# Taking both groups of heads for each half of the queries, in every block of a stack of graph attention layers

## The chip, the cores and the metric

The kernel runs on one core of one Trainium2 chip. Its time is the device time of one execution in microseconds (us). The profile is one execution of the program, recorded by the hardware profiler. PE is the matmul engine (PEld is its weight loading), DVE, ACT and POOL are the vector, scalar and GpSimd engines, and SP is the queue that issues nearly all DMAs here.

## The reference

Sixteen batches `x` of 1024 nodes with 128 features pass through three transformer layers whose attention is masked by one adjacency matrix, and then through one graph attention layer:

```python
# layers 0, 1, 2 (B=16, N=1024, 8 heads of 16)
Q, K, V = h @ Wq, h @ Wk, h @ Wv
scores = einsum('bnhd,bmhd->bhnm', Q, K) / sqrt(16)
attn = softmax(where(adj == 0, -inf, scores))
x = layer_norm(h + (einsum('bhnm,bmhd->bnhd', attn, V) @ Wo + bo), ln1_g, ln1_b)
x = layer_norm(x + relu(x @ W1 + b1) @ W2 + b2, ln2_g, ln2_b)
# layer 3
h = x @ W
e = leaky_relu((h @ a_src)[:, :, None] + (h @ a_dst)[:, None, :], 0.2)
out = layer_norm(softmax(where(adj == 0, -inf, e)) @ h + x)
```

## The kernel before

**Blocks and steps.** One block is the attention of one batch in one of the three layers; there are 48. The list `blocks` (line 651) takes four batches at a time: layer 0 of all four, layer 1 of all four, layer 2 of all four, then the next four batches. A block has 32 steps. A step (`score_step`, line 411) is four heads (one of two groups `g`) for one half of the queries (`qh`, 512 of 1024) against one tile of 128 keys (`kt`, 0 to 7). It makes the scores of two heads at a time on PE (line 419) into one of three PSUM slots; then either ACT takes the exponential (426) and POOL multiplies by the mask (427), or DVE adds the mask (429) and ACT takes the exponential (441). Which of the two depends on `kt` alone. Four steps later PE multiplies the exponentials with the values into one accumulator (line 446). After eight steps the accumulator of that (g, qh) is complete; `finish` (449) transposes it on DVE (457), takes reciprocals (459) and scales on POOL (460) into the tile `A`, which has one part for each half of the queries.

**The order in a block.** Before, the loops run group 0 with both halves, then group 1 with both halves; only the first and the last block run half 0 with both groups and then half 1 with both groups (line 757).

**Stacking.** PE multiplies in a form in which each float32 of a query or key is split in two parts, `hi` and `lo`. `split` (372) makes them from the projections, and `stack(m, g)` (397) lays rows of them into the tiles that line 419 reads: two tiles Wk and two Wq for a group of heads, each filled by 4 DMAs of 128 KB on SP (line 404). So one `stack` is 16 DMAs. The tags Wk and Wq have 4 buffers each: those of both groups of a block. A buffer can be filled again only when its last score matmul has read it.

`stack(m, 1)` is written at step 1 of block m (step 6 in block 0), `stack(m + 1, 0)` at step 19 of block m (step 24 in block 0); ahead of that line the projections of block m + 1 must have been made (`need(("proj", m + 1))`, line 781).

**What else runs in the steps.** Each step may also run one small task (`piece`, 682) from chains with due times: the projections of the next block (`proj_tasks`), what follows attention in the block before (`post_tasks`: transposing `A` at 473, output projection, two layer norms, feed-forward), and the last layer of a finished batch (`last_tasks`). In the last layer `rows_gh` (577) issues 16 small DMAs on SP (lines 589 and 590) whose rows the edge matmuls of line 603 read eight or more steps later, and `end` (630) issues the output (635).

**Who sets the order.** PE and ACT run in the order in which the code writes their instructions (line 754). The orders of DVE, POOL and SP are made by a planner at build time, which works with its own estimates of how long instructions take; at run time each engine and queue takes its own list strictly in that order. A DMA on SP that waits for a buffer holds up all DMAs behind it.

## Time and profile before

| | us |
|---|---|
| median of three runs | 4116.18 (4115.72 to 4121.67) |
| the profiled execution | 4115.92, its span 4114.1 |
| PE busy, weight loads apart | 3809.8 (93%) |
| DVE, ACT, POOL busy | 3405.7 (83%), 3393.8 (82%), 3445.6 (84%) |
| stacking DMAs issued by SP | 1536 of 128 KB |
| mean granted clock of PE | 0.98 of full speed |

A busy share is an average over the whole span. In ordinary blocks (76 us each, 2.4 us a step) a step needs about 0.66 us of PE for scores and 0.98 us for values, and the tasks fill the rest. Blocks that also carry the last layer take 80 to 102 us. In the views below, a line of the order in time gives start, duration, engine, line, operation, tiles and count, and in brackets how long the engine stood idle before and whom it waited for; a line of the waits gives total, number and longest.

### The profile page before, as it was taken

What the parts mean: (1) busy time and instruction counts of PE and PEld (TensorE: products, weight loads), DVE (VectorE), ACT (ScalarE), POOL (GpSimd) and SP (SyncE); (2) the same over time, 40 slices, a digit from 0 to 9 for tenths busy, and PEclk for the clock granted to TensorE, in tenths of its full rate; (3) what the DMA queues carried; (4) which work ended last, traced back from release to release, by engine and by line L of the source; (5) the groups of instructions that cost most, each with busy time, mean ns of one, the idle gap of its engine ahead of it and who ended that gap; (6) DMA issues with size and microseconds to landing.
All of it is one profiled execution on the core that took longest, in us unless ns stands there. A gap on an engine that the chain in (4) does not pass through costs nothing.

```text
span 4114.1 us, 107861 instructions
## 1 busy us (share of the span) xinstructions
PE 3809.8 (93%) x44501; PEld 1545.5 (38%) x44501; DVE 3405.7 (83%) x5326; ACT 3393.8 (82%) x3961; POOL 3445.6 (84%) x3010
## 2 busy tenths in 40 slices
PE   7999999999999999999999999999999999999996
PEld 2333333344443333334444333333434433333445
DVE  6888888888887888888888888888888888888874
ACT  7999999977778999997777899998777789999760
POOL 5888888888888888887888888888888888888884
PEclk8999999999999999999999999999999999999997
DMA  6221222222211221221222221221222112222100
GB/s 158 61 63 48 57 63 54 51 53 59 64 51 50 63 63 48 57 63 48 59 54 55 61 60 45 63 63 43 53 74 54 48 47 58 62 54 51 51 20 19
DMA packets 124465, 233.13 MB, mean 57 GB/s; under 512 B 34624, under 2 KB 73792, under 8 KB 123968
## 3 DMA queue, kind: packets, MB, share of 16 engines
q1 hardware_dynamic: 122960, 225.71, 21.9%
q8 instruction: 354, 5.80, 0.6%
q14 instruction: 143, 1.17, 0.1%
q10 hardware_dynamic: 1008, 0.44, 0.0%
HBM read 15.54 MB, written 8.39 MB: 6 GB/s over the span
## 4 chain that ended last, share of the span: by engine, by line
PE 49%; DVE 19%; ACT 12%; POOL 11%; issue 9%; ACTq 0%; DMA 0%; SPq 0%; DVEq 0%; POOLq 0%
PE t L293 19%; PE acc L446 15%; PE s L419 12%; DVE e L429 11%; POOL e L427 6%; ACT e L426 5%; ACT e L441 5%; DVE st L318 2%; PE t L282 2%; DVE lo L382 1%; POOL x L337 1%; DVE x L325 1%; ACT xT L287 1%; DVE tt L457 1%; POOL x L341 1%
## 5 line engine op out<-in xcount | busy, mean ns | idle before, releaser
L429 DVE TENSOR_TENSOR e<-s,mask_add 128x1024 f32<-128x1024 f32 x2112 | 2499.5, 1211 | 406.7 <-PE s L419 321.1
L441 ACT ACTIVATE e<-e 128x1024 f32<-128x1024 f32 x2112 | 2196.5, 1062 | 365.0 <-DVE e L429 340.0
L427 POOL TENSOR_TENSOR e<-e,mask 128x1024 f32<-128x1024 f32 x960 | 2048.6, 2149 | 391.3 <-ACT e L426 376.8
L446 PE MATMUL acc<-e,v 128*17 128x512 f32 x12288 | 1628.5, 602 | 63.4 <-DVE tt L457 32.6
L419 PE MATMUL s<-Wq,Wk 64*128 64x512 f32 x6144 | 1206.6, 458 | 83.4 <-ACT e L426 34.6
L426 ACT ACTIVATE e<-s 128x1024 f32<-128x1024 f32 x960 | 982.3, 1023 | 190.9 <-PE s L419 174.7
L419 PEld LDWEIGHTS s<-Wq,Wk 64*128 64x128 f32 x6144 | 499.3, 185 | 1068.9 <-DVE e L429 430.6
L446 PEld LDWEIGHTS acc<-e,v 128*17 128x17 f32 x12288 | 208.0, 95 | 578.6 <-issue 463.6
L337 POOL TENSOR_SCALAR x<-x,mv 128x128 f32<-128x128 f32 x896 | 389.2, 448 | 24.0
L341 POOL TENSOR_TENSOR x<-x,ln_g 128x1024 f32<-128x1024 f32 x97 | 229.3, 2364 | 33.3 <-PE t L282 33.3
L293 PE MATMUL t<-hd,e 128*32 128x129 f32 x8192 | 243.3, 276 | 4.7 <-DVE x L621 3.2
L335 POOL TENSOR_TENSOR mv<-mv,half_neg 128x4 f32<-128x4 f32 x224 | 231.9, 1035 | 18.5
L293 PEld LDWEIGHTS t<-hd,e 128*32 128x32 f32 x8192 | 226.1, 110 | 23.1 <-DVE x L325 4.9
L325 DVE TENSOR_TENSOR x<-t,x 128x512 f32<-128x512 f32 x192 | 131.7, 686 | 91.6 <-PE t L293 90.7
L293 PE MATMUL t<-x1T,W 128*32 128x512 f32 x1536 | 203.9, 603 | 3.0 <-ACT x1T L287 1.5
L318 DVE BATCH_NORM_STATS2 st<-x 128x6 f32<-128x128 f32 x896 | 196.7, 279 | 3.0
L282 PE MATMUL t<-identf,x 128*128 128x128 f32 x888 | 147.2, 289 | 55.2 <-DVE lo L382 27.2
L293 PEld LDWEIGHTS t<-W,hT 128*32 128x32 f32 x6144 | 172.5, 111 | 63.6 <-issue 26.3
L333 POOL TENSOR_SCALAR mv<-mv 128x4 f32<-128x4 f32 x224 | 52.8, 236 | 164.0 <-DVE mv L320 136.3
L293 PE MATMUL t<-W,hT 128*32 128x128 f32 x6144 | 187.1, 274 | 2.7 <-DVE x L325 1.9
L282 PEld LDWEIGHTS t<-identf,x 128*128 128x128 f32 x888 | 94.6, 142 | 250.0 <-issue 93.7
L606 DVE SCALAR_TENSOR_TENSOR e<-s,mask 128x1024 f32<-128x1024 f32 x128 | 150.5, 1209 | 4.8 <-PE s L603 4.1
(97 smaller groups left out, 2488.2 us busy)
## 6 DMA issues: line engine op xcount, KB each, us to landing
Wk<-hi SPq DMA_DIRECT2D x384, 128.0 KB
Wk<-lo SPq DMA_DIRECT2D x384, 128.0 KB
Wq<-hi SPq DMA_DIRECT2D x384, 128.0 KB
Wq<-lo SPq DMA_DIRECT2D x384, 128.0 KB
x<-in_x_dram SPq DMA_DIRECT2D x16, 512.0 KB
out_dram<-x SPq DMA_DIRECT2D x31, 256.0 KB
ai<-in_adj_dram SPq DMA_DIRECT2D x8, 512.0 KB
g_rows<-parts SPq DMA_DIRECT2D x120, 4.0 KB
```

The source lines that it names most:

```text
L282: nc.tensor.transpose(ps[:, t * P:(t + 1) * P], src[:, 4 * h + t, :], identf)
L293: nc.tensor.matmul(dst[j:j + SLOT, :], lhsT[:, j:j + SLOT], rhs, start=start, stop=stop)
L318: nc.vector.bn_stats(st[:, t, :], z[:, t, :])
L335: nc.gpsimd.tensor_tensor(v, v, half_neg[:, ts], OP.pow)
L337: nc.gpsimd.tensor_scalar(z[:, t, :], z[:, t, :], mv[:, t, 0:1], mv[:, t, 1:2], op0=OP.add, op1=OP.mult)
L341: nc.gpsimd.tensor_mul(z, z, rows(gain, n))
L419: nc.tensor.matmul(ps[:, r * 512:(r + 1) * 512], k[64 * r:64 * r + 64, kt * P:(kt + 1) * P], q[64 * r:64 * r + 64, q0:q0 + 512], start=Tru ...
L426: nc.scalar.activation(ev, psv, AF.Exp, scale=HD ** -0.5)
L427: behind["pool"] = nc.gpsimd.tensor_mul(ev, ev, m).ins
L429: behind["dve"] = nc.vector.tensor_add(ev, psv, m).ins
L441: nc.scalar.activation(ev, ev, AF.Exp, scale=HD ** -0.5)
L446: nc.tensor.matmul(acc[j * SLOT:j * SLOT + HD + 1, :], v_bufs[m % 2][:, kt, 2 * j + g, :], e[:, j, :], start=first, stop=last)
```

## The change

Every block now runs half 0 of the queries with both groups of heads and then half 1 with both, as the first and last block did. The `stack` of the next block's group 0 is written at step 24 in every block, five steps later than before in all but the first.

```diff
             order = [(g, qh) for g in range(G) for qh in range(2)]
-            if m in (0, len(blocks) - 1):
+            if True:
                 order.sort(key=lambda x: x[1])
...
-                    if at == (24 if m == 0 else 19):
+                    if at == 24:
                         need(("proj", m + 1))
                         stack(m + 1, 0)
```

## The prediction

> **What bounds the kernel now.** I read the busy line of the page first, then busy time by stretch (one ordinary block, then blocks 12, 13 and 14), then the waits of the DMA queue, and last the order in time on SP and PE. A step's place in time comes from PE's score matmuls (L419): 6144 of them, four to a step, in order, so the first of each four starts a step. I number blocks from 0 and the 32 steps of a block from 0.

> ```profile
> PE 3809.8 (93%) x44501; PEld 1545.5 (38%) x44501; DVE 3405.7 (83%) x5326; ACT 3393.8 (82%) x3961; POOL 3445.6 (84%) x3010
> ...
> 561.21:637.32 76.11, 71.65 (x724) 25.63 (x721) 65.36 (x97) 69.46 (x79) 66.97 (x57) 1.00 0.23 57
> 1062.70:1157.17 94.47, 89.00 (x1314) 42.93 (x1314) 79.93 (x139) 69.86 (x88) 75.55 (x73) 1.00 0.21 55
> 1157.17:1256.60 99.43, 93.34 (x1361) 44.16 (x1360) 81.03 (x136) 74.48 (x85) 82.76 (x77) 1.00 0.23 58
> ...
> SPq L404 <- PE s L419: 2018.2, 141, 32.7
> ```

> The columns of a stretch are its length and then PE, PEld, DVE, ACT, POOL busy. An ordinary block takes 76.1 us with PE busy 71.6; blocks 13 and 14, which also carry the last layer of earlier batches, take 94.5 and 99.4 with PE idle 5.5 and 6.1. So PE, fed in an order written by hand, sets the pace, and what stops PE costs time. The last line is the one that this change touches: SP, which issues the stacking DMAs (L404), stands at the head of its queue waiting for PE's score matmuls 141 times, 2018 us in all. The stacks are issued as soon as their target buffers are free, not when the loop reaches the line that writes them.

> [...]the tiles of step 0's first scores had their last issue end at 17.46 us and were read at 19.69 (at most 2.2 us), and those of its second scores had it end at 22.58 and were read at 25.53 (2.95 us, the wait named as a DMA). I take 2.2 for a landing and keep 2.95 as its upper end. [...]so a late stack stops all of PE. The trace agrees: in the 2.95 us wait above no other matmul ran. SP keeps its list in order too, as the views below show.

> **The change part by part.**

> *(a) Order of the halves.* The 32 steps do the same matmuls, masks and exponentials (which engine masks depends on kt alone). 46 blocks take them in another order. Removed 0, added 0. The four "finish" tasks still come at steps 11, 19, 27 and 35. Following the due times of the task chains by hand, every other task falls on the same step as before: none is forced earlier by the need for the projections at step 19 (their last piece falls at 18), so asking at 24 forces nothing either.

> *(b) When the buffers come free.* Tags Wk and Wq have 4 buffers, 2 per group of heads. Group 0's were last read at step 15 and are now last read at step 23. Group 1's still at step 31. So the next block's first stack starts 8 steps later (the written line moves 5 steps; the buffers decide).

> *(c) When the stacks are needed.* First stack: at step 32, as before. Second stack: at step 8 of its block, where it was 16.

> A stack is 16 DMAs on SP. In an ordinary block (here 5 into 6):

> ```profile
> 444.03 0.47 SPq L404 DMA_DIRECT2D Wk<-hi  x1
> ...
> 483.61 0.47 SPq L404 DMA_DIRECT2D Wk<-hi  x1
> ...
> 493.19 1.24 SPq L404 DMA_DIRECT2D Wq<-lo  x2
> ...
> 464.10 0.74 PE L419 MATMUL s<-Wq,Wk 64*128 64x512 f32 x4
> ...
> 485.08 0.73 PE L419 MATMUL s<-Wq,Wk 64*128 64x512 f32 x4
> ...
> 501.12 1.04 PE L419 MATMUL s<-Wq,Wk 64*128 64x512 f32 x4
> ```

> The three PE lines are steps 23 and 32 (= step 0 of block 6) and step 8. The second stack runs from 483.61 to 494.43, 10.8 us (median over the trace 11.0), so 0.67 us a DMA. New first stack: free at 464.8, issued by 476, landed by 478.2; needed at 485.1: 6.9 us spare. Second: landed by 494.43 + 2.2 = 496.6 (497.4 at 2.95); needed at 501.1: 3.7 to 4.5 spare; the tightest block has 6.4 us from last issue to step 8, so 3.4 to 4.2. Ordinary blocks: cost 0, hidden by PE's steps 23 to 31 and 0 to 7.

> *(d) The blocks with other work on SP.* Of the four groups of batches, three have heavy blocks after them (10 to 14, 22 to 26, 34 to 38). Each batch's last layer issues 16 small DMAs (rows_gh, L589/L590), 10.6 us of SP, and in-order. They come at steps 10, 16, 23 and 26 of blocks 10, 11, 12 and 13 (and so on by 12). At 10 and 16 SP is done with them by about step 22, before the stack is released. At 23 and 26 they now meet it, where before the stack had run at steps 15 to 20. Measured:

> ```profile
> 1042.08 0.74 PE L419 MATMUL s<-Wq,Wk 64*128 64x512 f32 x4
> ...
> 1061.30 0.77 PE L603 MATMUL s<-g_rows,h_rows 4*128 4x256 f32 x8
> ...
> 1063.83 0.50 PE L419 MATMUL s<-Wq,Wk 64*128 64x512 f32 x2 [0.63 <-DVE e L606]
> ...
> 1045.30 0.68 SPq L589 DMA_DIRECT2D g_rows<-parts  x1
> ...
> 1055.31 0.60 SPq L590 DMA_DIRECT2D h_rows<-parts  x1
> ...
> 1147.69 0.69 SPq L589 DMA_DIRECT2D g_rows<-parts  x1
> ```

> Which goes first is the planner's choice. Block 11 shows how it chooses:

> ```profile
> 927.49 0.59 SPq L404 DMA_DIRECT2D Wk<-lo  x1
> 930.67 0.69 SPq L589 DMA_DIRECT2D g_rows<-parts  x1
> ...
> 941.03 0.60 SPq L590 DMA_DIRECT2D h_rows<-parts  x1
> 941.67 1.16 SPq L404 DMA_DIRECT2D Wq<-hi  x2
> ```

> Four stack DMAs, then all sixteen of rows_gh (SP stood still 2.6 us for them), then the other twelve. What the fifth stack DMA reads was ready before the rows' data (ACT writes both in order, one step apart), so the planner counted an issue longer than it takes: four from step 15's release to the rows' readiness at step 17.4.

> *Block 12 (24, 36).* Release at 1042.08 + 0.74 + 0.2 = 1043.0. At that planner's pace three stack DMAs precede the rows (ready 1.3 steps later): rows from 1045.3 to 1055.9, the other 13 by 13 x 0.65 = 8.4, to 1064.3, landed 1066.5. The second scores of step 32 ran at 1063.83: 2.7 us late.

> *Block 13 (25, 37).* Step 23 began at 1136.3, release 1137.3; the rows are ready 10.4 us later, eight planned issues. Eight real ones end at 1142.5, SP stands until 1147.69, rows to 1158.6, eight more to 1163.8, landed 1166.0; the second scores of step 32 would have run at 1157.5: 8.5 us late. The second stack follows at once and lands by about 1177, step 8 being at 1183: no cost. Block 14's output and x DMAs (0.4 us each) meet 12 us of spare.

> Sum: 3 x (2.7 + 8.5) = 34 us of PE standing still. Of this the 5.5 to 6.1 us that PE idles in the following block can be regained at most, for PE runs ahead only as far as three score buffers: between 17 and 34 us remain. I take 24: 4114.1 + 24 = 4138 in the profile's terms. The profiled execution took 4115.9 and the median is 4116.2, so 2 more: **4140**.

> **Rivals.**

> *Stack first.* If all 16 of it precede the rows, block 13 has no stall (stack ends at 1148.3), and block 12 has stack to 1054.0, rows to 1064.7, landed 1066.9, against edge matmuls at 1061.30: 5.6 us, three times, 17 us at most; 10 after regain: 4126. For it: the release comes before the rows' data in both blocks. Against: block 11's order.

> *Hidden.* All of it fits: 4116 within 8 us. For it: ordinary blocks have the spare shown, and blocks 13 and 14 may lose their stall to waits that they have anyway. Against: in block 12, 32 DMAs from 1043.0 cannot land before 1066 in any order. This is also the case where the change does nothing.

> *Faster.* The first half's attention is complete after the finish at step 19, not 27, so its transpose (L473, 0.70 us on DVE, at 411.06 in block 5, in a stretch where DVE has no pause) can go to steps 20 to 25, where DVE waits for PE (6.9 us a block). Bound 0.70 x 47 = 33 us: 4083. It decides if DVE alone holds PE at steps 0 to 5. Against: ACT does two 1.06 us exponentials a step there, 2.1 us, more than DVE's share.

> *Planner worse.* It sees stacks longer than they are (above), so at steps 0 and 8 it plans with PE standing and may order DVE and POOL worse in heavy blocks, which exceed ordinary ones by 91 us a group. A tenth to a quarter of 273 us: 27 to 68 on top of the forecast, 4165 to 4210.

> **How the numbers follow.** Interleaved 0.34 (4128 to 4155), stack first 0.24 (4116 to 4134), hidden 0.17, faster 0.15, planner worse 0.10. 0.2% is 8 us, about what a measurement of this kernel can tell from no change (its three runs span 6). Slower: 0.34 + 0.14 + 0.10 = 0.58; same: 0.10 + 0.17 = 0.27; faster 0.15. The range 4100 to 4165 takes in the first three, a third of the faster case and a little of the last. The slower cases alone: 4125 to 4165.

> **What would show it.** (b): first stacks begin right after step 23's scores. (c): PE never waits for a stack at step 8, and ordinary blocks stay at 76.1. (d): new waits of PE for a DMA at step 0 of blocks 13, 14, 25, 26, 37, 38, and L404 split by L589 in 12 and 13. Wrong if ordinary blocks change length: then DVE's or POOL's order moved, which I hold at zero; or if those stalls are there and the heavy blocks are no longer.

## The result and the profile after

| | before | changed |
|---|---|---|
| median, us (4 runs each) | 4118.15 (4115.72 to 4121.67) | 4136.63 (4134.81 to 4142.12) |
| span of the profiled execution, us | 4114.1 | 4134.3 |

The changed kernel is slower: the ratio of its time to that before is 1.0046, with a 95% interval of 1.0029 to 1.0064. Forecast were 4140 us and a ratio of about 1.006.

The first view is the page's busy line, then busy time by stretch for blocks 7, 13 and 14 (length; PE, PEld, DVE, ACT, POOL busy; the clock granted to PE, as a share; DMA share; GB/s), then two lines of the waits of SP and of PE, all of the changed kernel.

```profile
PE 3814.5 (92%) x44501; PEld 1546.7 (37%) x44501; DVE 3403.4 (82%) x5326; ACT 3395.2 (82%) x3961; POOL 3451.0 (83%) x3010
```

```profile
563.29:639.43 76.14, 71.67 (x725) 25.63 (x722) 65.25 (x97) 69.50 (x79) 67.11 (x57) 1.00 0.23 57
1067.41:1167.33 99.92, 91.00 (x1313) 43.22 (x1313) 80.00 (x139) 69.73 (x87) 75.28 (x73) 0.97 0.23 62
1167.33:1266.83 99.50, 93.39 (x1361) 44.17 (x1360) 81.06 (x136) 74.49 (x85) 82.93 (x78) 1.00 0.22 58
```

```profile
SPq L404 <- PE s L419: 2021.2, 124, 51.9
...
PE s L419 <- DMA Wk<-hi: 13.2, 3, 4.6
```

The busy line says nearly nothing: no engine's share moved by more than one point of a hundred. The stretches say where to look. The ordinary block has its old length (76.14 for 76.11), block 14 too (99.50 for 99.43), and block 13 went from 94.47 to 99.92, with a granted clock of 0.97 where it was 1.00. The last line is new: three times PE's score matmuls wait for a stack, 13.2 us in all, in the first step of blocks 13, 25 and 37. Before, they waited for one at the start of the kernel alone.

In SP's order in time, block 12 shows why (of the row DMAs, L589 and L590 in turn, only the first and the last L589 are shown):

```profile
1047.00 0.48 SPq L404 DMA_DIRECT2D Wk<-hi  x1
1047.57 0.99 SPq L404 DMA_DIRECT2D Wk<-lo  x1
1049.65 0.69 SPq L589 DMA_DIRECT2D g_rows<-parts  x1
...
1058.95 0.63 SPq L589 DMA_DIRECT2D g_rows<-parts  x1
1060.27 0.53 SPq L404 DMA_DIRECT2D Wk<-hi  x1
...
1067.98 1.24 SPq L404 DMA_DIRECT2D Wq<-lo  x2
1069.31 0.55 SPq L404 DMA_DIRECT2D Wk<-hi  x1
```

and PE's order in time at the same place:

```profile
1067.41 0.49 PE L419 MATMUL s<-Wq,Wk 64*128 64x512 f32 x2 [0.62 <-DVE e L429]
1071.94 0.80 PE L419 MATMUL s<-Wq,Wk 64*128 64x512 f32 x2 [4.04 <-DMA Wk<-hi]
1072.67 1.91 PE L446 MATMUL acc<-e,v 128*17 128x512 f32 x8
1074.35 1.93 PE L293 MATMUL t<-x1T,W 128*32 128x512 f32 x8
```

Step 23's scores release the buffers, the stack begins at 1047.0, two of its DMAs go out, then sixteen row DMAs, then the other fourteen, whose last issue ends at 1069.2. SP stands 1.0 us for the rows' data ahead of 1049.65, and the third stack DMA, behind them in its list, goes out at 1060.27, though step 23's scores had ended at 1047.16. The second scores of step 32 wait for it until 1071.9. The matmuls after the wait take nearly twice their usual time (1.91 us for eight of L446, else 1.05).

Taken from each block's first score to the next block's, the 20.1 us between the profiles are: blocks 13, 25 and 37, 5.5 + 6.3 + 4.7 = 16.5; blocks 10, 22, 34 and 46, 2.0 + 0.9 + 0.8 + 1.8 = 5.5; all other blocks together -1.9. A block can differ by some us between two profiles without a stall: in the profile of the kernel with line 24 alone (below), whose time is that of before, block 13 is 1.5 us longer than here before, block 14 3.0 longer and block 37 1.5 shorter. PE ran at half its clock for one or two stretches of some 3.4 us there in the one and not in the other (last section). So differences of up to 3 us in one block of one profile show nothing by themselves.

### The profile page after: what moved, and what is told of

Its sections match the earlier page's. It is cut to its first block, busy times and chain, and to the rows that moved or that the text cites. A ratio compares the mean times of both kernels' runs of the same rounds, so it can differ in the third digit from the quotient of the medians.

```text
span 4134.3 us, 107834 instructions
## 1 busy us (share of the span) xinstructions
PE 3814.5 (92%) x44501; PEld 1546.7 (37%) x44501; DVE 3403.4 (82%) x5326; ACT 3395.2 (82%) x3961; POOL 3451.0 (83%) x3010
## 3 DMA queue, kind: packets, MB, share of 16 engines
q1 hardware_dynamic: 122960, 225.71, 21.5%
q14 instruction: 142, 1.16, 0.1%
## 4 chain that ended last, share of the span: by engine, by line
PE 47%; DVE 19%; ACT 13%; POOL 12%; issue 9%; SPq 0%; DMA 0%; ACTq 0%; DVEq 0%; POOLq 0%
PE t L293 18%; PE acc L446 15%; PE s L419 11%; DVE e L429 10%; POOL e L427 6%; ACT e L441 5%; ACT e L426 5%; DVE st L318 2%; POOL x L337 2%; PE t L282 2%; DVE lo L382 1%; ACT xT L287 1%; DVE x L325 1%; DVE tt L457 1%; POOL mv L335 1%
## 5 line engine op out<-in xcount | busy, mean ns | idle before, releaser
L446 PE MATMUL acc<-e,v 128*17 128x512 f32 x12288 | 1630.9, 603 | 65.4 <-DVE tt L457 32.7
L419 PE MATMUL s<-Wq,Wk 64*128 64x512 f32 x6144 | 1209.1, 459 | 97.4 <-ACT e L426 37.8
L419 PEld LDWEIGHTS s<-Wq,Wk 64*128 64x128 f32 x6144 | 499.9, 185 | 1084.2 <-issue 440.6
L446 PEld LDWEIGHTS acc<-e,v 128*17 128x17 f32 x12288 | 208.1, 95 | 582.4 <-issue 472.5
L335 POOL TENSOR_TENSOR mv<-mv,half_neg 128x4 f32<-128x4 f32 x224 | 232.2, 1037 | 18.5
L502 ACT ACTIVATE hT<-t,b 128x512 f32<-128x512 f32 x192 | 134.4, 700 | 27.3 <-PE t L293 26.8
```

The costliest lines, as they stand in the source:

```text
L335: nc.gpsimd.tensor_tensor(v, v, half_neg[:, ts], OP.pow)
L419: nc.tensor.matmul(ps[:, r * 512:(r + 1) * 512], k[64 * r:64 * r + 64, kt * P:(kt + 1) * P], q[64 * r:64 * r + 64, q0:q0 + 512], start=Tru ...
L446: nc.tensor.matmul(acc[j * SLOT:j * SLOT + HD + 1, :], v_bufs[m % 2][:, kt, 2 * j + g, :], e[:, j, :], start=first, stop=last)
```

## The experiments

Each is compared with the kernel before in runs of its own session, as a ratio with its 95% interval; the medians of before were 4122.5, 4124.0 and 4116.5 in the three sessions. Two theories stood at the start. One: SP's queue is too full at three places, where the stack, now released at step 23, meets the row DMAs. The rival: the planner's orders changed all over the program, and the loss is the sum of many small ones.

**The order undone in three blocks.**

```diff
-            if True:
+            if m % 12 or not m:
...
-                    if at == 24:
+                    if at == (19 if m and m % 12 == 0 else 24):
```

> The new order in every block but 12, 24 and 36, which take the old order with the stack at step 19. Theory (SP collision in these three blocks: the stack for the next block, released at step 23, meets the 16 row DMAs): the waits of PE for a stack at step 0 of blocks 13, 25 and 37 go, and with them 5.4 + 6.0 + 4.4 = 16 us of the 20 us between the two profiles; about 4118 us, and some 3 us more than before stay. Rival (many small changes of the planner's orders all over the program): two or three blocks of 46 give back next to nothing, about 4133 to 4136.

Measured: 4126.3 us, ratio 1.0016 (1.0009 to 1.0023). The three waits for a stack are gone, and two thirds of the loss: 46 blocks were changed, undoing three brings back 0.30%. What stays is 0.16% or some 6.6 us by the ratio, 3.8 us between the medians, where 3 were expected. In this kernel's profile blocks 10, 22, 34 and 46 are 2.1 + 1.1 + 2.2 + 2.0 = 7.4 us longer than before; nothing else is longer by a like amount in every group. In each of the four, steps 1 to 5 make up 0.7 to 0.8 us of it, and DVE's order is another there (see the sum, below); the rest lies in steps 20 to 22, where PE ran at half its clock for 3.41 us.

**The order in those three blocks alone.**

```diff
-            if m in (0, len(blocks) - 1):
+            if m % 12 == 0 or m == len(blocks) - 1:
...
-                    if at == (24 if m == 0 else 19):
+                    if at == (24 if m % 12 == 0 else 19):
```

> The kernel before with the new order and the stack at step 24 in blocks 12, 24 and 36 alone. Theory (SP collision): the three stalls are there in full, 16 us: about 4132 to 4134. Rival (spread over all blocks): within 3 us of before, about 4118.

Measured: 4132.5 us, ratio 1.0030 (1.0019 to 1.0040): +12.4 us by the ratio, 9.9 between the medians; blocks 13, 25 and 37 are 6.8 + 6.1 + 4.2 us longer. The waits of PE and its order in time at block 13:

```profile
PE s L419 <- DMA Wk<-lo: 13.6, 3, 4.7
```

```profile
1063.28 0.78 PE L603 MATMUL s<-g_rows,h_rows 4*128 4x256 f32 x8
1064.68 0.50 PE L419 MATMUL s<-Wq,Wk 64*128 64x512 f32 x2 [0.63 <-DVE e L429]
1069.80 0.80 PE L419 MATMUL s<-Wq,Wk 64*128 64x512 f32 x2 [4.62 <-DMA Wk<-lo]
1070.53 1.91 PE L446 MATMUL acc<-e,v 128*17 128x512 f32 x8
1072.21 1.93 PE L293 MATMUL t<-x1T,W 128*32 128x512 f32 x8
```

By the ratios the stalls make some two thirds of the loss, from both sides; by the medians, 9.9 of 18.5 us when they are put in, and 14.7 when they are taken out. And a stall costs more than its wait: the matmuls before this one ran at their usual pace, those after it at about half (1.91 us for eight of L446, else 1.05).

**Stack ahead of the row DMAs.**

```diff
-                        stack(m + 1, 0)
+                        with tc.high_priority(offset=SOON) if m % 12 == 0 else nullcontext():
+                            stack(m + 1, 0)
```

> The changed kernel, with the stack written in blocks 12, 24 and 36 at a higher priority, so that on SP all 16 of its DMAs come before the 16 row DMAs instead of 2 before and 14 after. Theory (SP has 32 issues of 0.65 us, 21 us, between step 23's release and the first use of either result some 18 us later, whatever their order): PE stands still at the edge matmuls of step 31 of these blocks instead, some 5 us each, and the time stays at 4130 to 4138. Rival (only the planner's interleaving is at fault): the stall is gone, about 4118 to 4121.

Measured: 4138.8 us, ratio 1.0040 (1.0027 to 1.0054). The wait moved to the edge matmuls, as the waits of PE show:

```profile
PE s L603 <- DMA h_rows<-parts: 10.2, 3, 3.6
```

Blocks 12, 24 and 36 are now 4.4, 4.7 and 2.2 us longer, 13 and 25 still 1.4 and 1.6, as they are with the order undone, where no stall is. The interval overlaps that of the changed kernel. So neither order is shown to be cheaper: it is not the planner's interleaving that costs, but that 32 issues stand between step 23 and the first use of what they bring, and the order decides which matmul waits.

**Half of the row DMAs issued from ACT.**

```diff
-                queue = nc.scalar if r and b >= B - 2 else nc.sync
+                queue = nc.scalar if r and (b >= B - 2 or b % 4 == 2) else nc.sync
```

> The changed kernel, with 8 of the 16 row DMAs of every third batch of four issued from ACT's queue instead of SP's; the same bytes move. Theory (the issue time of SP is what lacks): SP gets 8 x 0.65 = 5.2 us back in blocks 12, 24 and 36, more than the 4.0 us that PE waited, so the waits vanish; ACT spends about 5 us three times in blocks where it has 20 us of idle time; 4117 to 4123. Rival (the transfers themselves, or their landing, are late): the waits stay, 4134 or more.

Measured: 4146.1 us, ratio 1.0057 (1.0043 to 1.0071); the time expected was missed by 23 us. The waits for the stack shrank from 13.2 to 2.6 us in four waits, so the time that the row DMAs take on SP was what lacked; but blocks 12, 24 and 36 are 9.2, 6.7 and 6.2 us longer. The changed kernel's busy time by stretch agrees: while SP issued the sixteen row DMAs, and then the other fourteen of the stack, it was (the last three numbers are PE's clock, the DMA engines' busy share and GB/s)

```profile
1049.65:1060.20 10.55, 9.79 (x72) 3.15 (x68) 9.60 (x11) 10.50 (x12) 10.29 (x12) 1.00 0.03 10
1060.27:1069.20 8.93, 6.83 (x54) 1.99 (x50) 6.86 (x7) 8.22 (x11) 8.66 (x5) 1.00 0.70 172
```

The rows took 0.66 us each with the DMA engines 3% busy, so moving their bytes is not what took the time. For the stack, with 70%, issuing and moving are not told apart here. In the kernel with half the rows on ACT, ACT's order in time, and PE's:

```profile
1052.69 1.52 ACTq L589 DMA_DIRECT2D g_rows<-parts  x1
...
1058.68 0.71 ACTq L590 DMA_DIRECT2D h_rows<-parts  x1
1059.44 1.02 ACT L426 ACTIVATE e<-s 128x1024 f32<-128x1024 f32 x1 [6.78 <-DMA g_rows<-parts]
```

```profile
1060.52 1.22 PE L419 MATMUL s<-Wq,Wk 64*128 64x512 f32 x4 [4.07 <-ACT e L426]
```

Eight issues in a row keep ACT from its exponentials for 6.8 us, and PE, three score buffers ahead at most, stands for 4.1. The expectation counted ACT's idle time over the block; what counts is that these issues come in one piece. The time of the issues is what counts here: 0.66 us each on SP in the rows, and moving half of them to ACT was paid with ACT's own time, the 6.8 us above.

**The written line of the stack alone.**

```diff
-                    if at == (24 if m == 0 else 19):
+                    if at == 24:
```

on the kernel before, with its order of halves.

> The kernel before with its old order of the halves, and the stack for the next block written at step 24 in every block: the second edit alone. Theory (a stack starts when the buffers' last read is done, step 15 in this order, wherever it is written; only its rank on SP against the row DMAs of steps 16 and 23 can change): same as before within 4 us, first stacks still issued right after step 15. Rival (the written step sets the start): stacks start at step 24 or later and the three stalls appear, 16 us more than before.

Measured: 4121.8 us, ratio 0.9996 (0.9987 to 1.0004): no difference. SP's order in time in block 12:

```profile
1025.44 0.47 SPq L404 DMA_DIRECT2D Wk<-hi  x1
...
1035.29 2.08 SPq L404 DMA_DIRECT2D Wq<-lo  x2
1046.82 0.69 SPq L589 DMA_DIRECT2D g_rows<-parts  x1
```

The stack is still issued right after step 15 and is done 9 us ahead of the rows, though its line now stands at step 24. The DMAs' place in the source was not their time.

**The new order in ordinary blocks alone.**

```diff
-            if True:
+            if m % 12 not in late or not m or m == len(blocks) - 1:
...
-                    if at == 24:
+                    if at == (19 if m and m % 12 in late else 24):
...
+    late = (9, 10, 11, 0, 1, 2)
```

> The new order in the blocks without last-layer work alone; blocks 9 to 14, 21 to 26, 33 to 38, 45 and 46 keep the old order and step 19. Theory (ordinary blocks hide the later stacks and the moved transpose of A gains nothing, and what is left beside the three stalls sits in the heavy blocks): within 3 us of before, ordinary blocks 76.1 us. Rival (the 6 us that stayed with the order undone in three blocks are spread over ordinary blocks): 6 us over before. Rival (the earlier transpose helps): up to 20 us under before.

Measured: 4121.9 us, ratio 0.9998 (0.9990 to 1.0006): no difference. By this edit blocks 1 and 2 keep the old order too, so that 24 of the 46 changed blocks have the new one. In these no loss is found (the interval leaves at most 0.06%, some 2.5 us), so it comes from the other 22, most of which carry last-layer work. The rival that expected a gain finds none here: the interval leaves at most 0.1%, some 4 us. In the changed kernel the transpose of A did move (order in time of DVE, at the end of block 5, step 24):

```profile
469.08 0.70 DVE L473 STREAM_TRANSPOSE aT<-A 128x512 f32<-128x512 f32 x1
```

It left the start of the next block, and that block is not shorter.

**Stack first, and later edges.**

```diff
+                        with tc.high_priority(offset=SOON) if m % 12 == 0 else nullcontext():
+                            stack(m + 1, 0)
...
-                (2, rows_gh, ""), (8, edges(0), ""),
+                (2, rows_gh, ""), (12 if b % 4 == 2 else 8, edges(0), ""),
```

> The changed kernel with the stack ahead of the row DMAs in blocks 12, 24 and 36, and the first edge matmuls of every third batch of four 12 steps after the row DMAs instead of 8. Theory (SP capacity): the stack lands by step 28 and the rows some 10 us before they are read, so that PE has no wait for a DMA in these blocks: 10 to 16 us less than with the stack first alone, so 2 to 8 us over before, as long as the later tasks that this shifts fit. Rival (the time is lost elsewhere and the stalls only cover it): no gain over the changed kernel.

Measured: 4178.8 us, ratio 1.0134 (1.0119 to 1.0150). Expected were 2 to 8 us over before, found are 55. Blocks 12, 24 and 36 are now 0.6 to 1.7 us shorter than before and PE has no wait for a DMA there, so the stall is gone; but every later task of that batch slides, and blocks 13 and 14 are 8.0 + 8.0 us longer, 25 and 26 8.3 + 8.2, 37 and 38 6.0 + 3.9. In blocks 14, 26 and 38 the next batch's row DMAs now come too late for their edges, some 3 us each. This doesn't count for the rival, since the shifted tasks are a second change.

**What follows attention, by halves.** The new order completes the first half of the queries at step 19. Three kernels use it, with the tasks of a half spaced 1, 1, 3 steps, then 3, 3, 5, then 2, 5, 7.

```diff
+            elif g == G - 1 and qh == 0:
+                halves[:] = post_tasks(b, l)[1]
+                halves.append(put(halves[0], ("half", b, l)))
             elif g == G - 1 and qh == 1:
-                post = post_tasks(b, l)[0]
-                chain = put(post[:1], ("attn", b, l))
+                post, chain = halves[1], halves[2]
+                chain = put(post[:1], ("attn", b, l), chain if any(c is chain for c in chains) else None)
```

> The changed kernel, with a use of the new order: what follows attention (transpose of A, output projection, norms, feed-forward) runs in two halves, the first from step 19 of the same block on, since the first half of the queries is then complete; the last block already does so. In ordinary blocks PE's steps 26 to 37 hold no tasks before, 1.65 to 2.3 us each, and steps 8 to 25 hold all of them, 2.5 to 3.4 us. Theory (PE's load would be spread): ordinary blocks fall from 76.1 towards the 72 us that PE is busy, by 1 to 3 us each, 40 to 120 us in all. Rival (ACT is the bound in the steps without tasks, with two exponentials of 1.06 us each a step): nothing gained, or a loss where the halves wait for POOL's two smaller steps.

> As after_attention_by_halves, with the tasks of a half further apart: 3 steps from the end of its attention to the transpose, 3 to the output projection, 5 to the transpose of the normed rows (were 1, 1 and 3). Theory (that kernel lost its time because PE, in order, stood at output projections for DVE's transpose, 246 + 183 us, and at the next transposes for POOL's norm, 121 us): most of the 310 us comes back, 4110 to 4200, and ordinary blocks of 76 us or less show whether spreading gains anything. Rival (spreading costs by itself: tasks in steps where ACT is the bound): ordinary blocks stay at 80 us or more, 4300 and up.

> The same with 2, 5 and 7 steps. Theory: PE's waits for the transpose and the norm are gone altogether, and the time is within 30 us of the variant with 3, 3 and 5, on the better side if those waits were not gone there; it may lose in heavy blocks, where the chains take longer and last-layer tasks crowd the following blocks. Rival: as there.

Measured: 4429.5 us, ratio 1.0742 (1.0720 to 1.0764); 4206.3, 1.0217 (1.0200 to 1.0234); 4213.0, 1.0232 (1.0215 to 1.0249). The waits of PE's weight loads in the first of them:

```profile
PEld t L293 <- DVE aT L473: 245.6, 69, 7.4
...
PEld t L282 <- POOL x L337: 121.4, 174, 6.7
```

With room between the tasks most of this came back, if not quite to the 4200 us expected at most, but not the gain: ordinary blocks, 83.0 us in the first kernel, take 78.3 and 76.8, never less than 76.1. One of them, of the kernel with 3, 3, 5:

```profile
579.64:657.99 78.35, 72.09 (x724) 25.49 (x720) 65.02 (x97) 70.07 (x79) 67.49 (x59) 1.00 0.22 55
```

PE's busy time is the same to 1%, and its idle time grew from 4.5 to 6.3 us. Spreading the tasks gains nothing here. That ACT bounds the steps without tasks is the reason argued for; no run showed it by itself.

No kernel tried is faster than the kernel before.

## Why the prediction was right, and where it was not

**(a), (b), (c) held.** The changed kernel's first stacks begin right after step 23's scores (in block 5 they end at 466.67 for the first pair of heads and 466.90 for the second, and the stack, whose first tiles the first pair reads, starts at 466.74), PE never waits for a stack at step 8, and ordinary blocks keep their 76.1 us. In block 6 the second stack's last issue ends at 496.66 and step 8 starts at 503.21; 3.7 to 4.5 us were said to be spare, and 4.3 are, with 2.2 for the landing.

**(d) Block 12: right place, sizes off.** Forecast: three stack DMAs, the rows, thirteen more, second scores of step 32 late by 2.7 us, of which two thirds would stay. Found: two, sixteen, fourteen, and the scores are 3.4 us late at block 13: a wait of 4.0 us replaced one of 0.63 (the landing took 2.7 us, not 2.2, and one more issue stood behind the rows). The 2.2 rested on the start of the kernel, whose other landing, 2.95 us, is the last part of a wait of 5.34. The block's first step grew by 5.4 us: the matmuls after the wait lost some 2 us to a lower clock, which the working had at nothing. (At block 37 the step grew by 4.4 only, from 4.91 us to 9.32, since the profile before has a stretch of lower clock there; at 13 and 25 it took 3.40 before.) Nothing was regained: the other 31 steps of block 13 have the lengths they had before, to 0.1 us in all. The allowance of a third for regaining was wrong: in these blocks PE's idle time was no reserve. That it lies at waits which a later start moves along is a reading, not shown by a run.

**(d) Block 13: wrong.** The forecast had the planner put eight stack DMAs ahead of the rows and the stack 8.5 us late. It put all sixteen there (order in time of SP):

```profile
1147.07 0.47 SPq L404 DMA_DIRECT2D Wk<-hi  x1
...
1156.32 1.23 SPq L404 DMA_DIRECT2D Wq<-lo  x2
1157.85 0.69 SPq L589 DMA_DIRECT2D g_rows<-parts  x1
```

They end at 1157.55, ten microseconds before step 32. The step that failed is the planner's pace, taken as constant from one place in block 11: four issues between a release and the rows. It gave three for two in block 12, eight for sixteen in block 13, and with it 3 x 8.5 = 25.5 us of standing still that are not there.

**The sum was right with terms that were not, which is luck.** 3 x (2.7 + 8.5) less a third gave 24 us; found are 16.5 us in three stalls, of some 5.5 us each instead of 2.7, no stall in block 13, and 5.5 us in blocks 10, 22, 34 and 46 that no step of the prediction had. Of these, 3.0 us are another order that the planner gives DVE. At step 1 of block 10 it now puts a node product (L571) ahead of a masked score, and DVE waits for ACT (order in time of DVE):

```profile
798.27 0.56 DVE L571 TENSOR_TENSOR hd<-t,col 128x384 f32<-128x384 f32 x1 [1.06 <-ACT col L568]
```

Before, the same product came after the next score and did not wait. Steps 1 to 5 take 0.7 to 0.8 us more in each of the four blocks. The order undone in three blocks keeps this part, the new order in ordinary blocks alone, which has the old order in these four, has none of it. The rest, some 2.5 us, is nearly all in blocks 10 and 46: their steps 20 and 21 take 7.15 us, where they took 5.68 before, since PE ran at half its clock for 3.41 us there; block 22 takes 7.16 in both profiles and block 34 5.66, by the same stretch or its absence. Profiles of kernels with the old order in these blocks have this stretch in none or one of the four, with the new order in two to four; whether the new order makes it likelier was not tested.

**The rivals.** "Stack first" as an order cost the same as the interleaving within the noise, and not the 10 us that were forecast for it: the run that forced it is at 1.0040. "Hidden" holds for the ordinary blocks. "Faster" fell: the transpose moved and gained nothing. "Planner worse" is there with the 3.0 us of DVE's order, a tenth of its lower size.

## What to carry to other kernels

When a buffer comes free later, follow the queue that refills it: count the issues that stand between the release and the first use, other users' too, times the time of one issue, add a landing, and compare with the steps in between. Here 32 x 0.65 us and 2 to 3 us more stood against 19 us to the first edge matmuls and 21.5 to the second scores; neither the order of the issues nor the line where they are written decided. A queue that has room on average can lack it at three places in 48, and moving the issues to a busy engine moved the stall there. Price a stall of PE with the slow matmuls after it (about 2 us after a wait of 4 here), do not count on idle time elsewhere to win it back, and before you give a reason for a small difference in one block, look at the clock of both profiles there.

## What the runs showed of the hardware that I had not expected

A stall was followed by slow matmuls: at the three stalls of the changed kernel the clock granted to PE was at half for 6.83 us each, from 1069.50, 2083.26 and 3097.02 us on. At the first of them PE stood from 1067.90 to 1071.94 us. Busy time by stretch around it (the number after POOL's is the clock):

```profile
1066.09:1069.50 3.41, 1.06 (x8) 0.48 (x6) 3.41 (x4) 2.70 (x4) 3.22 (x3) 1.00 0.82 202
1069.50:1072.92 3.42, 0.98 (x6) 0.47 (x10) 0.17 (x2) 0.50 (x1) 1.75 (x1) 0.50 0.78 216
1072.92:1076.33 3.41, 3.41 (x18) 0.51 (x10) 1.18 (x1) 0.00 (x0) 0.00 (x0) 0.50 0.70 193
1076.33:1079.74 3.41, 3.41 (x28) 1.04 (x32) 2.22 (x3) 3.39 (x5) 1.71 (x1) 1.00 0.74 199
```

In the first stretch PE was busy for 1.06 us, and the second ran at half clock; in the second for 0.98, and the third, in which PE never stood, ran at half clock too; after that third the clock was whole again. So the clock was one stretch of 3.41 us behind what PE did here, and the slow matmuls came when the wait was over: eight of L446 took 1.91 us where else they take 1.05. That added about 2 us to a wait of 4. After ACT's issues, where PE stood 4.07 us, they took 1.91 too. A wait of 4 us is not needed: before the change PE waited 2.18 us for DVE in block 12, up to 1000.63, and the 3.41 us from 1000.96 on were at half clock. The kernel with the order undone in three blocks has such a stretch at block 13 with no wait for a DMA at all, which costs 1.4 us.
